# Factors of a tile copied across partition blocks by ScalarE, in place of a TensorE product with a mask

## The chip, the cores and the metric

The kernel runs on one core of one Trainium2 chip. The metric is the device time of one execution in microseconds (us). A core has five engines that work side by side, each through its own list of instructions in order: TensorE (PE; its weight loads are listed as PEld), VectorE (DVE), ScalarE (ACT), GpSimd (POOL) and SyncE (SP, which here only issues transfers). An instruction that needs another engine's result waits for it, and everything behind it on the same engine waits too. SBUF and PSUM are the on-chip memories, both with 128 partitions; matmuls write into PSUM.

## The reference, cut to what matters

The input `x` is 384 x 384 x 128 in float32. Two layers follow each other. The first is a triangle product with gates:

```python
z_n = _layernorm(z, norm_g, norm_b)              # over the 128 channels of each (row, column)
a = _linear(z_n, Wa, ba) * sigmoid(_linear(z_n, Wga, bga))
b = _linear(z_n, Wb, bb) * sigmoid(_linear(z_n, Wgb, bgb))
x = einsum('bijd,bjkd->bikd', a, b)              # per channel d a 384x384x384 product
x = _layernorm(x, normo_g, normo_b)
return z + _linear(x, Wo, bo) * sigmoid(_linear(z_n, Wgo, bgo))
```

The second layer computes gated projections of each row of that result, a sum over the row, an output projection, a residual and a layer norm. The change lies in the first layer norm, so only the first lines bear on it: every (row, column) needs a factor 1/sqrt(variance + eps), which multiplies its 128 channels before five projections.

## The kernel before, in words

The kernel has three stages. The first (to about 1280 us of the span) normalises `x`, projects it five times, and writes A and B (the factors of the triangle product), G (the output gate) and Z (the residual) to memory. The second multiplies A and B channel by channel. The third applies everything else, row by row. The change touches the first stage alone.

**Tiles and steps.** The first stage walks through 72 tiles (`NT`). A tile is 128 rows (on the partitions) by 16 columns (`CX`) by 128 channels. Each tile is worked through in four steps (`TS = 4`) of four columns (`CT = 4`); a step is called `s`, its tile `n`, its place in the tile `t` (0 to 3). The function `step(s)` writes the instructions out in this order, and no scheduler changes it: four projections `pga`, `pa`, `pgb`, `pb` of 128 x 512 on TensorE (L314), a sigmoid of `pga` and one of `pgb` on ScalarE (L322, `sga` and `sgb`), the gate of the step before on ScalarE (L264, `gt`), the two products `at` (L335) and `bt` (L351) on VectorE, the fifth projection `pgo` in four matmuls (L277), and its bias on VectorE (L279, `gs`). At the end of the step VectorE and GpSimd normalise the data of the step after next (`normalise_turned(s + 2)`, L219 and L223).

**Two ways to normalise.** The first three tiles (`OLD = 3`) are normalised with rows on the partitions and then turned by TensorE (`turn`, L249) and copied out by ScalarE (`turned_out`, L257). From tile 3 on, the kernel loads `x` a second time already turned, so that channels lie on the partitions and rows along the free axis. The mean is folded into the weights. The factor of a row must then multiply a column of the turned data, and must stand on all 128 partitions.

**How the factor gets there.** VectorE takes statistics (L160). At `t == 0` of tile `n`, GpSimd works out the factors of tile `n + 1` (`turned_factors`, L181 to L187; the last of them is a power, L187), one column of 16 factors for each row, on the partition of the row: the tile `rstd`, 128 x 16. What the later transposes need is `again`, 128 x 64: in each of the four blocks of 32 partitions, the factors of all four blocks of 32 rows. Then the 32 x 32 block transposes of VectorE (L219) yield rows along the free axis on every partition. To make `again`, GpSimd multiplies `rstd` by a mask `of_block` into `apart` (L190; each row's factor stands only in the column of its own block). In `repeat` at `t == 2`, TensorE multiplies `apart` by a constant matrix `alike` (L200; it adds up partitions that are equal modulo 32, so that every block gets all four), and ScalarE copies the 128 x 64 result from PSUM to `again` (L203). The PSUM tile is one of the two of the pool `p1t`, which the transposes `pevery` use too.

**What sets the order around it.** On ScalarE a step has `sga`, `gt`, `sgb` in this order, and at `t == 2` L203 between `gt` and `sgb`. On GpSimd a tile has, in order: the L223 product of step 0, the factors, L190, the store of G (issued at `gt`), the products of the next steps, `residual` (L242, one instruction of 4.5 us, at `t == 1`) with its store of Z, and the store of A at `t == 3`. The projections use six PSUM buffers (`p1p`) and a step uses five, so TensorE can run about one step ahead of the engines that empty them. In step 9, the first that repeats anything in the changed kernel, the turning of the old tiles still goes on: ScalarE's L257 copy of step 10's data stands at the end of step 9.

Of the kernel before, what the change touches and what calls it, by code (L numbers as in the profile page):

```python
# [9 lines left out]
FP = mybir.dt.float32  # L10
AF = mybir.ActivationFunctionType
ALU = mybir.AluOpType
# [8 lines left out]
def kernel(ctx: ExitStack, tc: tile.TileContext, ins, out: bass.AP):  # L21
# [17 lines left out]
    P = 128  # L39
# [71 lines left out]
    with tc.tile_pool(name="wprep", bufs=6) as wp, tc.tile_pool(name="p1s", bufs=3) as ps, tc.tile_pool(  # L111
# [4 lines left out]
        name="p1p", bufs=6, space=PSUM  # L116
    ) as ppp:
        tiles, turned, bts, gated, b_out_of = {}, {}, {}, {}, []
        alike = wp.tile([P, P], FP, tag="alike", name="alike", bufs=1)
        of_block = wp.tile([P, P // SQ], FP, tag="of_block", name="of_block", bufs=1)  # L120

        def place(n):
            rb, c = divmod(n, N // CX)
# [6 lines left out]
        def fetch_parts(n, parts):  # L130
            if n >= NT:
                return
            r0, c0 = place(n)
            xt = px.tile([P, CX, C], FP, tag="xt", name=f"xt_{n}")
            tiles[n] = {
                "x": xt,
                "st": ps.tile([P, CX, 6], FP, tag="st", name=f"st_{n}"),
                "rstd": ps.tile([P, CX], FP, tag="rstd", name=f"rstd_{n}"),
                "off": ps.tile([P, CX], FP, tag="off", name=f"off_{n}"),
            }  # L140
            if n < OLD:
                tiles[n]["mv"] = ps.tile([P, CX, 2], FP, tag="mv", name=f"mv_{n}")
            else:
                tiles[n]["apart"] = ps.tile([P, CX, P // SQ], FP, tag="apart", name=f"apart_{n}", bufs=1)
                tiles[n]["again"] = ps.tile([P, CX, P // SQ], FP, tag="again", name=f"again_{n}", bufs=2)
            for k in range(0, CX, CX // parts):
                nc.sync.dma_start(
                    out=xt[:, k : k + CX // parts, :], in_=x[r0 : r0 + P, c0 + k : c0 + k + CX // parts, :]
                )
                yield  # L150
# [26 lines left out]
        def turned_factors(n, c0, c1):  # L177

            st, v, d = (tiles[n][k][:, c0:c1] for k in ("st", "rstd", "off"))
            g = nc.gpsimd  # L180
            g.tensor_tensor(d, st[:, :, 1], st[:, :, 4], ALU.subtract)  # L181
            g.tensor_tensor(v, st[:, :, 2], st[:, :, 5], ALU.add)
            g.tensor_tensor(d, d, d, ALU.mult)
            g.tensor_scalar(d, d, C / 4.0, None, ALU.mult)
            g.tensor_tensor(v, v, d, ALU.add)
            g.tensor_scalar(v, v, 1.0 / C, EPS, ALU.mult, ALU.add)
            g.tensor_tensor(v, v, mhalf[:, 0 : c1 - c0], ALU.pow)  # L187
            if c1 == CX:
                v = tiles[n]["rstd"]
                g.tensor_tensor(  # L190
                    tiles[n]["apart"], v[:, :, None].to_broadcast([P, CX, P // SQ]),
                    of_block[:, None, :].to_broadcast([P, CX, P // SQ]), ALU.mult,
                )

        def repeat(n):

            if n >= NT:
                return
            again = ppt.tile([P, CT, P], FP, tag="ptr", name=f"pagain_{n}")[:, 0, 0 : CX * P // SQ]
            nc.tensor.matmul(  # L200
                again, lhsT=alike, rhs=tiles[n]["apart"].rearrange("p c b -> p (c b)"), start=True, stop=True
            )
            nc.scalar.copy(tiles[n]["again"].rearrange("p c b -> p (c b)"), again)  # L203

        def normalise_turned(s):
            n, t = divmod(s, TS)
# [86 lines left out]
        def step(s):  # L293
            n, t = divmod(s, TS)
            r0, c0 = place(n)
            if t == 0:
                if n >= OLD:
                    fetch(n + 3)
                fetch_turned(n + 2)
                if s >= CATCH_UP:  # L300
                    norm_factors(n + 1)
                tiles[n]["at"] = pa_.tile([P, CX, P], FP, tag="at", name=f"at_{n}")
                if c0 % CG == 0:
                    bts[n // TG] = (pb_ if (NT - 1 - n) // TG % 2 else pb_held).tile(
                        [P, P, CG], FP, tag="bt", name=f"bt_{n}"
                    )
            at, bt = tiles[n]["at"], bts[n // TG]
            k0 = c0 % CG + t * CT
            zT = turned[s]
            ahead = (n + 1, t - 1) if t else (n, TS - 1)  # L310

            def proj(k):
                pk = ppp.tile([P, CT, P], FP, tag="pk", name=f"p{k}_{s}")
                nc.tensor.matmul(pk, lhsT=wT[k], rhs=zT, start=True, stop=True)  # L314
                return pk

            def by_rows(p):
                return p.rearrange("d c r -> d r c")

            def sigmoid(k, pg, by_row=False):  # L320
                sg = ps.tile([P, P, CT] if by_row else [P, CT, P], FP, tag="sg", name=f"sg{k}_{s}")
                nc.scalar.activation(sg, by_rows(pg) if by_row else pg, AF.Sigmoid, bias=bcol["g" + k])  # L322
                return sg

            statistics(columns_ahead(s), columns_ahead(s + 1))
            for factors in FIRST_FACTORS.get(s, ()):
                norm_factors(*factors)
            pga, pa = proj("ga"), proj("a")
            if s == 0:
                nc.tensor.matmul(biases[:, 1, :], lhsT=nb_w, rhs=raw["go"], start=True, stop=True)  # L330
                nc.vector.tensor_tensor(gate_bias, biases[:, 1, :], gate_bias, ALU.add)
            sga = sigmoid("a", pga)
            if 0 < s <= S2:
                gate(s - 1)
            nc.vector.scalar_tensor_tensor(  # L335
                at[:, t * CT : (t + 1) * CT, :], pa, bcol["a"], sga, ALU.add, ALU.mult
            )
            if t == TS - 1:
                nc.gpsimd.dma_start(out=A[:, c0 : c0 + CX, r0 : r0 + P], in_=at)
            if t == 2 and n + 1 >= OLD:  # L340
                repeat(n + 1)
            pgb = proj("gb")
            sgb = sigmoid("b", pgb, by_row=True)
            if s + 1 < OLD * TS:
                turn(s + 1)
                turned_out(s + 1)
            if s == 0:
                normalise(0, 2)
            normalise(*ahead)
            pb = proj("b")  # L350
            nc.vector.scalar_tensor_tensor(  # L351
                bt[:, :, k0 : k0 + CT], by_rows(pb), bcol["b"], sgb, ALU.add, ALU.mult
            )
            if s < S2:
                gate_project(s)
            if s + 2 >= OLD * TS:
                normalise_turned(s + 2)
            if s < CATCH_UP:
                if s in FIRST_RESIDUALS:
                    residual(FIRST_RESIDUALS[s])  # L360
                if s in FIRST_FETCHES:
                    fetch(FIRST_FETCHES[s])
            elif t == 1:
                residual(n + 1)
            if k0 + CT == CG and n < NT - 1:
                b_out_of.extend((bt, r0, c0 + CX - CG, k) for k in range(0, P, BR))
            if t == TS - 1 and b_out_of:
                bt, r0, k0, r = b_out_of.pop(0)
                nc.sync.dma_start(out=B[:, k0 // CG, r0 + r : r0 + r + BR, :], in_=bt[:, r : r + BR, :])
# [10 lines left out]
        def of_the_turned():  # L380

            nc.vector.tensor_scalar(center, ident, -1.0 / C, None, ALU.add)
            yield
            for some in (("ga", "a"), ("gb", "b", "go")):
                centred = ppp.tile([P, CT, P], FP, tag="pk", name="centred_" + some[0])
                for n, k in enumerate(some):
                    nc.tensor.matmul(centred[:, n, :], lhsT=center, rhs=wT[k], start=True, stop=True)
                for n, k in enumerate(some):
                    nc.scalar.copy(wT[k], centred[:, n, :])
                yield  # L390
            nc.gpsimd.memset(of_block, 0.0)
            for k in range(P // SQ):
                nc.gpsimd.memset(of_block[k * SQ : (k + 1) * SQ, k : k + 1], 1.0)
            few = wp.tile([P, SQ], FP, tag="few", name="few", bufs=1)
            nc.vector.tensor_tensor(few, ident[:, 0:SQ], ident[:, SQ : 2 * SQ], ALU.add)
            for k in (2, 3):
                nc.vector.tensor_tensor(few, few, ident[:, k * SQ : (k + 1) * SQ], ALU.add)
            nc.vector.tensor_copy(
                alike.rearrange("p (b r) -> p b r", r=SQ), few[:, None, :].to_broadcast([P, P // SQ, SQ])
            )  # L400
            yield

        def last_weights():

# [661 lines left out]
```

## Time and profile before

| what | us |
|---|---|
| median of 3 runs (3215.39 to 3218.23) | 3218.12 |
| the profiled execution, its own time | 3217.2 |
| its span, first to last instruction | 3215.4 |
| TensorE busy in the span | 3184.3 |
| VectorE, GpSimd, ScalarE busy | 2714.7, 2436.2, 1793.2 |
| in the 1000 us from 300 to 1300: TensorE, VectorE, GpSimd, ScalarE busy | 994.57, 892.14, 799.21, 434.30 |
| share of the transfer engines' time in that window, GB/s | 0.92, 353 |
| granted TensorE clock | 0.998 |

How to read it: a line of a timeline gives the start in us from the start of the span, the time from the first start to the last end of what the line merges, the engine, the line of the code, the operation, output<-inputs, the shapes and the count; a bracket at the end says how long the engine had been idle just before, and what ended that. In a group of instructions, the two numbers after the count are the busy time in all and the mean duration in ns, and then the idle time before it. Durations of instructions that follow each other on one engine can overlap[...]. So the time that an engine is held by an instruction is the distance between two starts, and not the duration.

### The profile page before, as it was taken

To read this page: it belongs to the slowest core of one execution; us is meant where nothing else is said; L and a number is where in the kernel's file an instruction comes from. 1 tells how busy PE (TensorE), PEld (TensorE's weight loads), DVE (VectorE), ACT (ScalarE), POOL (GpSimd) and SP (SyncE) were. 2 spreads that over 40 slices of the span, in tenths; PEclk is the share of its full clock that TensorE was granted. 3 is DMA by queue.
4 is the path that set the end of the run, shared out by engine and by line. 5 is a ranking of instruction groups with operands and counts; after the bars stand their busy time and mean duration, and the time that the engine had idled before them with its cause. 6 is when DMAs were issued, how large, how long until landed. Compare 5 with 4: busy or idle time off the path is not lost.

```text
span 3215.4 us, 50848 instructions
## 1 busy us (share of the span) xinstructions
PE 3184.3 (99%) x14681; PEld 2103.1 (65%) x14681; DVE 2714.7 (84%) x8317; ACT 1793.2 (56%) x4190; POOL 2436.2 (76%) x2187
## 2 busy tenths in 40 slices
PE   9999999999999999999999999999999999999998
PEld 5555555555555554655555555788888888888886
DVE  7899999999999997455555555999999999999999
ACT  6444444444444444222222222588888888888888
POOL 7788888888888887455555555499999998888888
PEclk9999999999999999999999999999999999999999
DMA  6989999999999998999999999777777777777774
GB/s 236 353 342 361 366 362 365 355 360 345 368 359 363 366 355 287 368 319 313 312 311 308 311 311 303 253 254 261 272 258 261 269 261 258 270 260 259 268 264 160
DMA packets 419189, 982.72 MB, mean 306 GB/s; under 512 B 30288, under 2 KB 326352, under 8 KB 373728
## 3 DMA queue, kind: packets, MB, share of 16 engines
q1 hardware_dynamic: 377984, 752.64, 67.4%
q0 software_dynamic: 40352, 226.57, 17.8%
q8 instruction: 119, 1.95, 0.2%
q14 instruction: 158, 1.29, 0.1%
q10 hardware_dynamic: 576, 0.26, 0.0%
HBM read 526.39 MB, written 452.98 MB: 305 GB/s over the span
## 4 chain that ended last, share of the span: by engine, by line
PE 96%; POOL 1%; ACT 1%; DVE 1%; DMA 1%; issue 0%; SPq 0%; POOLq 0%; ACTq 0%; DVEq 0%
PE pm L699 23%; PE py L539 8%; PE pf L809 8%; PE pleft L835 8%; PE pg L837 8%; PE pga L314 7%; PE pgb L314 7%; PE pgo L277 7%; PE pa L314 7%; PE pb L314 7%; PE ptr L562 4%; POOL rstd L187 0%; PE pagain L200 0%; PE pg L848 0%; POOL acc L242 0%
## 5 line engine op out<-in xcount | busy, mean ns | idle before, releaser
L699 PE MATMUL pm<-ab 128*128 128x384 f32 x2304 | 745.8, 487 | 2.1 <-DVE gs L279 2.1
L719 POOL TENSOR_TENSOR acc<-acc,xd 128x384 f32<-128x384 f32 x381 | 380.8, 1000 | 362.6 <-DVE xd L712 362.4
L699 PEld LDWEIGHTS pm<-ab 128*128 128x128 f32 x2304 | 438.1, 190 | 307.3 <-DVE gs L279 2.7
L322 ACT ACTIVATE sga<-pga,c_L_conv_bga 128x512 f32<-128x512 f32 x288 | 198.0, 688 | 550.1 <-PE pga L314 550.0
L712 DVE TENSOR_TENSOR xd<-pm,acc 128x384 f32<-128x384 f32 x381 | 212.2, 557 | 344.2 <-POOL acc L719 320.1
L717 ACT ACTIVATE sq<-xd 128x384 f32<-128x384 f32 x381 | 188.5, 495 | 541.2 <-DVE xd L712 541.1
L827 ACT ACTIVATE res<-res,off,rs 128x128 f32<-128x128 f32 x1134 | 474.8, 485 | 1.4
L545 DVE SCALAR_TENSOR_TENSOR py<-py,acc,gr 128x128 f32<-128x128 f32 x1152 | 416.7, 362 | 0.9
L277 PEld LDWEIGHTS pgo<-wT_go,xT 128*128 128x128 f32 x2208 | 287.5, 192 | 124.8 <-issue 78.9
L550 DVE BATCH_NORM_STATS2 st<-res 128x6 f32<-128x128 f32 x1128 | 338.8, 300 | 0.0
L860 POOL TENSOR_TENSOR res<-res,r_L_conv_ln_bias 128x1536 f32<-128x1536 f32 (+1 forms) x96 | 326.7, 3403 | 7.5
L859 POOL TENSOR_TENSOR res<-res,r_L_conv_ln_scale 128x1536 f32<-128x1536 f32 (+1 forms) x96 | 326.9, 3406 | 0.7 <-ACT res L827 0.5
L242 POOL TENSOR_TENSOR acc<-xt,r_L_conv_b_out 128x2048 f32<-128x2048 f32 x72 | 326.5, 4535 | 0.0
L223 POOL TENSOR_TENSOR xT<-every,xT 128x256 f32<-128x256 f32 x276 | 202.6, 734 | 155.3 <-DVE every L219 152.1
L539 PE MATMUL py<-w_o,xr 128*128 128x128 f32 x2304 | 320.0, 275 | 0.0
L809 PE MATMUL pf<-w_o,h 128*128 128x128 f32 x2280 | 316.7, 275 | 0.0
L835 PE MATMUL pleft<-pairT,m_L_conv_W_left 128*128 128x384 f32 x768 | 311.5, 487 | 0.4 <-ACT pairT L563 0.4
L837 PE MATMUL pg<-pairT,m_L_conv_W_gate 128*128 128x384 f32 x768 | 310.6, 486 | 0.0
L842 ACT ACTIVATE sg<-pg,c_L_conv_b_gate 128x384 f32<-128x384 f32 x384 | 223.2, 581 | 150.4 <-PE pg L837 101.5
L351 DVE SCALAR_TENSOR_TENSOR bt<-pb,c_L_conv_bb,sgb 128x512 f32<-128x512 f32 x288 | 216.2, 751 | 97.3 <-PE pb L314 93.2
L314 PE MATMUL pga<-xT,wT_ga 128*128 128x512 f32 x552 | 284.0, 596 | 7.6 <-POOL xT L223 7.5
L539 PEld LDWEIGHTS py<-w_o,xr 128*128 128x128 f32 x2304 | 288.4, 192 | 0.8
(195 smaller groups left out, 6537.7 us busy)
## 6 DMA issues: line engine op xcount, KB each, us to landing
Z<-acc POOLq DMA_DIRECT2D x72, 1024.0 KB, 10.4
A<-at POOLq DMA_DIRECT2D x72, 1024.0 KB, 14.1
G<-gt POOLq DMA_DIRECT2D x72, 1024.0 KB, 10.2
gr<-G SPq DMA_DIRECT2D x96, 768.0 KB, 5.8
zr<-Z SPq DMA_DIRECT2D x96, 768.0 KB, 7.3
xr<-X SPq DMA_DIRECT2D x96, 768.0 KB, 8.2
X<-xd SPq DMA_DIRECT2D x381, 192.0 KB, 5.7
xt<-in_x_dram SPq DMA_DIRECT2D x71, 1024.0 KB, 7.5
```

Of the source, the lines that this page charges most:

```text
L277: nc.tensor.matmul(pgo[:, c, :], lhsT=zT[:, c, :], rhs=wT["go"], start=True, stop=True)
L314: nc.tensor.matmul(pk, lhsT=wT[k], rhs=zT, start=True, stop=True)
L539: nc.tensor.matmul(py[:, q, :], lhsT=g["x"][:, i, q * P : (q + 1) * P], rhs=w_o0, start=True, stop=True)
L545: nc.vector.scalar_tensor_tensor(py[:, q, :], py[:, q, :], rs0[:, q, u : u + 1], g["g"][:, i, q, :], ALU.mult, ALU.mult)
L550: nc.vector.bn_stats(b["st"][:, k, q, :], b["res"][:, k, q, :])
L699: nc.tensor.matmul(products[d, ib].rearrange("p (s c) -> p s c", c=CG), lhsT=ab[:, 0, q, ib * P : (ib + 1) * P], rhs=b_of(d)[:, :, q, :], ...
L719: nc.gpsimd.tensor_tensor(s1[:, ib, :], s1[:, ib, :], xd, ALU.add)
L809: nc.tensor.matmul(pf[:, q, :], lhsT=h[:, q * P : (q + 1) * P], rhs=w_o, start=True, stop=True)
L827: nc.scalar.activation(g["res"][:, i, q, :], g["res"][:, i, q, :], AF.Identity, bias=g["off"][:, i, q : q + 1], scale=g["rs"][:, i, q : q ...
L835: nc.tensor.matmul(pleft, lhsT=w_left, rhs=pairT, start=True, stop=True)
L837: nc.tensor.matmul(pg[:, 0:N], lhsT=w_gate, rhs=pairT, start=True, stop=True)
L859: nc.gpsimd.tensor_tensor(flat, flat, over(ln_s, n * NB), ALU.mult)
```

## The change

`apart`, `of_block` and `alike` go, with the instructions that make them. `repeat` copies on ScalarE instead: for each of the four blocks of 32 rows and each of the four blocks of 32 partitions, one copy of 32 partitions x 16 elements from `rstd` to a strided place in `again`, sixteen in a tile. It moves from `t == 2`, ahead of the third projection, to `t == 1`, behind the sigmoid `sgb`. In program order it then stands ahead of `turn(s + 1)` and `turned_out(s + 1)` where a step still has them. Only the first of the sixteen copies waits (for GpSimd's `rstd`); the other fifteen wait for nothing.

```diff
@@ norm_factors / turned_factors
             g.tensor_tensor(v, v, mhalf[:, 0 : c1 - c0], ALU.pow)
-            if c1 == CX:
-                v = tiles[n]["rstd"]
-                g.tensor_tensor(
-                    tiles[n]["apart"], v[:, :, None].to_broadcast([P, CX, P // SQ]),
-                    of_block[:, None, :].to_broadcast([P, CX, P // SQ]), ALU.mult,
-                )
 
         def repeat(n):
 
             if n >= NT:
                 return
-            again = ppt.tile([P, CT, P], FP, tag="ptr", name=f"pagain_{n}")[:, 0, 0 : CX * P // SQ]
-            nc.tensor.matmul(
-                again, lhsT=alike, rhs=tiles[n]["apart"].rearrange("p c b -> p (c b)"), start=True, stop=True
-            )
-            nc.scalar.copy(tiles[n]["again"].rearrange("p c b -> p (c b)"), again)
+            for b in range(P // SQ):
+                for to in range(P // SQ):
+                    nc.scalar.copy(
+                        tiles[n]["again"][to * SQ : (to + 1) * SQ, :, b], tiles[n]["rstd"][b * SQ : (b + 1) * SQ, :]
+                    )
@@ step
-            if t == 2 and n + 1 >= OLD:
-                repeat(n + 1)
             pgb = proj("gb")
             sgb = sigmoid("b", pgb, by_row=True)
+            if t == 1 and n + 1 >= OLD:
+                repeat(n + 1)
             if s + 1 < OLD * TS:
                 turn(s + 1)
                 turned_out(s + 1)
@@ of_the_turned
                 for n, k in enumerate(some):
                     nc.scalar.copy(wT[k], centred[:, n, :])
                 yield
-            nc.gpsimd.memset(of_block, 0.0)
-            for k in range(P // SQ):
-                nc.gpsimd.memset(of_block[k * SQ : (k + 1) * SQ, k : k + 1], 1.0)
-            few = wp.tile([P, SQ], FP, tag="few", name="few", bufs=1)
-            nc.vector.tensor_tensor(few, ident[:, 0:SQ], ident[:, SQ : 2 * SQ], ALU.add)
-            for k in (2, 3):
-                nc.vector.tensor_tensor(few, few, ident[:, k * SQ : (k + 1) * SQ], ALU.add)
-            nc.vector.tensor_copy(
-                alike.rearrange("p (b r) -> p b r", r=SQ), few[:, None, :].to_broadcast([P, P // SQ, SQ])
-            )
-            yield
```

More of the change, by code (lines that the diff above doesn't have):

```diff
@@ L118 @@
         tiles, turned, bts, gated, b_out_of = {}, {}, {}, {}, []
-        alike = wp.tile([P, P], FP, tag="alike", name="alike", bufs=1)
-        of_block = wp.tile([P, P // SQ], FP, tag="of_block", name="of_block", bufs=1)
         def place(n):
@@ L143, in fetch_parts @@
             else:
-                tiles[n]["apart"] = ps.tile([P, CX, P // SQ], FP, tag="apart", name=f"apart_{n}", bufs=1)
                 tiles[n]["again"] = ps.tile([P, CX, P // SQ], FP, tag="again", name=f"again_{n}", bufs=2)
```

## The prediction, made before the changed kernel ran

> **What bounds the kernel now.** I read the page first (who is busy in the stage that the change touches), then the chain that ended last, then one tile of the first stage engine by engine.
>
> ```profile
> PE 96%; POOL 1%; ACT 1%; DVE 1%; DMA 1%; issue 0%; SPq 0%; POOLq 0%; ACTq 0%; DVEq 0%
> ```
>
> TensorE holds the end of the program: whatever makes its list shorter in the first stage shows in full, unless a wait takes its place. Now one tile of the first stage, TensorE's timeline:
>
> ```profile
> 608.58 1.02 PE L314 MATMUL pga<-xT,wT_ga 128*128 128x512 f32 x2
> ...
> 612.91 1.02 PE L314 MATMUL pga<-xT,wT_ga 128*128 128x512 f32 x2
> 613.77 1.02 PE L314 MATMUL pa<-xT,wT_a 128*128 128x512 f32 x2
> 614.62 0.33 PE L200 MATMUL pagain<-apart,alike 128*128 128x64 f32 x2
> 614.79 1.08 PE L314 MATMUL pgb<-xT,wT_gb 128*128 128x512 f32 x2
> ...
> 617.46 1.02 PE L314 MATMUL pga<-xT,wT_ga 128*128 128x512 f32 x2
> ```
>
> A plain step lasts 612.91 - 608.58 = 4.33 us, with no gap. The step with L200 lasts 617.46 - 612.91 = 4.55 us. So L200 costs TensorE 0.22 us in each tile, on the path. ScalarE in the same steps:
>
> ```profile
> 611.36 0.69 ACT L322 ACTIVATE sgb<-pgb,c_L_conv_bgb 128x512 f32<-128x512 f32 x1 [0.45 <-PE pgb L314]
> 614.03 0.69 ACT L322 ACTIVATE sga<-pga,c_L_conv_bga 128x512 f32<-128x512 f32 x1 [1.98 <-PE pga L314]
> 614.61 0.62 ACT L264 ACTIVATE gt<-gs 128x512 f32<-128x512 f32 x1
> 615.13 0.20 ACT L203 COPY again<-pagain 128x64 f32<-128x64 f32 x1
> 615.91 0.69 ACT L322 ACTIVATE sgb<-pgb,c_L_conv_bgb 128x512 f32<-128x512 f32 x1 [0.57 <-PE pgb L314]
> ```
>
> The new copies follow the `sgb` at 611.36 (`t == 1`). ScalarE is idle 1.98 us there, then waits for TensorE again: it has 2.4 us of spare time in a step. GpSimd:
>
> ```profile
> 607.90 2.94 POOL L187 TENSOR_TENSOR rstd<-rstd,mhalf 128x16 f32<-128x16 f32 x1
> 610.91 0.29 POOL L190 TENSOR_TENSOR apart<-rstd,of_block 128x64 f32<-128x64 f32 x1
> 611.15 0.64 POOL L267 DMA_DIRECT2D G<-gt  x1
> 611.81 0.74 POOL L223 TENSOR_TENSOR xT<-every,xT 128x256 f32<-128x256 f32 x1
> 614.23 0.73 POOL L223 TENSOR_TENSOR xT<-every,xT 128x256 f32<-128x256 f32 x1 [1.67 <-DVE every L219]
> ```
>
> The product at 611.81 ends at 612.55, and TensorE needs it at 612.91: GpSimd is only 0.36 us ahead at `t == 2`. That is the tightest place beside TensorE's own.
>
> **The change part by part.**
>
> *L200 goes.* 0.22 us in each of the 66 tiles in which TensorE sets the pace: -14.5 us. In the last three tiles (no fifth projection there, it comes later) TensorE waits for GpSimd's L223, so there only GpSimd's gain counts.
>
> *L190 goes.* It holds GpSimd some 0.27 us (it lasts 0.29, and the next starts 0.24 after it). In most tiles that is cover: the 0.36 us become 0.6. On the path it counts where TensorE waits for the L223 behind it: two early tiles (waits of 1.88 us at 82.13 and 1.64 us at 156.56) and the last three (1.04 and 0.94 us in two of them). 5 x 0.27 = -1.3 us.
>
> *The setup goes* (five memsets and four VectorE instructions, 1.4 us in all, near 53 us). VectorE's next product there starts without a wait, TensorE's step 7 is not held by it: 0. *L203 and the PSUM buffer go*: ScalarE had time, and `pevery` loses a neighbour: 0.
>
> *Sixteen copies come, per tile.* The trace has no ScalarE instruction on 32 partitions, so I bound one. Nearest in shape is a 128x16 activation, SBUF to SBUF:
>
> ```profile
> 3197.02 0.22 ACT L995 ACTIVATE root<-ident 128x16 f32<-128x16 f32 x1
> 3197.14 1.25 ACT L827 ACTIVATE res<-res,off,rs 128x128 f32<-128x128 f32 x3
> ```
>
> The next starts 0.12 us after it, though it lasts 0.217 us: lower end 16 x 0.122 = 1.95 us. The Trainium skill has a rule against it: "VectorE: DVE Perf Modes", section "Two Vector instructions with no wait between them", says that a VectorE instruction whose output starts in another block of 32 partitions than the last one's starts only when all earlier ones are finished. The copies change that block every time. The rule is for VectorE; no run here shows whether ScalarE does it. If so, nothing overlaps: 16 x 0.217 = 3.5 us, and with the lost overlap of 0.095 us as a new start cost besides, 16 x 0.31 = 5.0 us, an estimate. So 1.95 to 5.0. I take 1.95, the row, since the rule names another engine.
>
> *What 1.95 or 3.5 us do.* The copies start when `sgb` lets go, 611.36 + 0.58 (the distance from `sga` to `gt`) = 611.94. GpSimd's power has ended at 610.84, so the first copy doesn't wait; in nearly all tiles the power is 1.2 us ahead. They end at 613.9 or 615.4; `sga`, next in the queue, was due at 614.03. At 3.5 it is 1.4 us late. VectorE's `at` waits for it, but stands at 615.64 anyway, and `sga` ends by 616.1: 0.5 us late. TensorE needs `at` only when its buffer comes round, at `pgb` of the next step, 2.5 us after `at` normally ends. `again` is needed first by L219 at 618.0. So both are hidden.
>
> *Where it stops being hidden.* Let the copies take C. Then `sgb` of `t == 2` ends at 613.7 + C, and behind it on VectorE stand `bt`, `gs`, three instructions of L219/L223, the statistics, `at` and so on with hardly a gap: by start distances the L219 for the product that GpSimd does ahead of the factors ends at about 619.4 + C. From there GpSimd needs 0.7 (product), 1.6 (six small ones), 2.9 (power), 0.7 (store of G) and 0.8 (product) = 6.8 us, to 626.2 + C. TensorE wants that product at 612.91 + 4 x 4.33 = 630.2. So up to C = 4.0 us (0.25 us a copy) TensorE sees nothing; each us beyond can cost up to a us a tile.
>
> *The one place without cover: step 9.* The first copies (tile 3) stand ahead of ScalarE's copy of step 10's data:
>
> ```profile
> 59.42 1.67 POOL L187 TENSOR_TENSOR rstd<-rstd,mhalf 128x8 f32<-128x8 f32 x1
> 59.89 0.58 ACT L257 COPY zn<-ptr 128x512 f32<-128x512 f32 x1
> ...
> 61.23 1.02 PE L314 MATMUL pga<-zn,wT_ga 128*128 128x512 f32 x2
> ```
>
> L257 ran at 59.89. Now ScalarE waits for the power's end at 61.09, copies for 1.95, and only then does L257 (0.58): TensorE's `pga` starts at 61.15 + 1.95 + 0.58 + 0.08 = 63.76 in place of 61.23, +2.5 us (+4.1 at 3.5). GpSimd's chain behind waits for VectorE's L219 of step 10, which follows TensorE, so nothing gives this back.
>
> *Sum:* -14.5 - 1.3 + 2.5 = -13.3 us against the profiled execution's 3217.2 (its span is 3215.4, the rest lies around it unchanged): 3203.9. The median lies 0.9 above: 3204.8. With C = 3.5 it would be 3206.4. Prediction: 3205.
>
> **The rivals.**
>
> *The copies cost 0.3 us each (slower).* ScalarE restarts from nothing at each block change, so C = 4.8, and the wait moves through VectorE to GpSimd's factors and TensorE's `pga` at `t == 2`. 0.8 us beyond the 4.0; since a stalled TensorE also moves the next tile's deadline back, I count half: 66 x 0.4 = +26, step 9 adds 5.4 in all: 3218 - 14.5 - 1.3 + 5.4 + 26 = 3234. For it: the rule above; ScalarE's copies here write three other blocks and come back, sixteen times. Against: 0.31 needs both the full 0.217 and a start cost. It decides from 0.28 us a copy on.
>
> *Another engine sets the pace (no change).* The transfer engines are busy for 0.92 of the window at 353 GB/s; a tile moves six times 1 MB in 17.53 us. If that rate is a ceiling, tiles stay at 17.53 us, and only the start's +2.5 and the last tiles' gain remain: 3219. Against it: slices of the same window move up to 412 GB/s, and TensorE's chain has no wait for a transfer. Copies at 0.27 to 0.29 us land here too.
>
> *GpSimd is late with the factors*, and ScalarE waits at the first copy with `sga` and `gt` behind it. Four of 69 tiles have the power after `sgb`, by up to 1.1 us, and in these TensorE was stalled by GpSimd already: at most +3 us, 3208, inside the forecast.
>
> **How the numbers follow.** A measurement of this kernel tells about 0.2%, 6.4 us, from no change: faster is under 3211.7, slower over 3224.6. Copies under 0.26 us with the pace still TensorE's: 66%, 3202 to 3211. No change (ceiling, or copies near 0.28): 12%. Slower (copies of 0.29 and over): 22%, of which about half lies under 3235. The range reaches from a start that is given back (3202 less 1) into that case: 3201 to 3234; the likeliest case alone has 3202 to 3209.
>
> **What would show it.** Right: plain steps of 4.33 us at every `t`, tiles of 17.32; copies starting 0.12 us apart; `sga` after them at once or up to 1.5 us late; `pga` of step 10 some 2.5 us later; L223 ahead of `pga` at `t == 2` with 0.6 us to spare. Wrong: copies starting 0.25 us or more apart, VectorE waiting for `sgb` at `t == 2`, TensorE waiting for GpSimd's L223 in the middle tiles, or tiles that stay at 17.5 us with nothing but transfers behind.

## The result, and the profile after

| | median us | ratio to before, 95% interval |
|---|---|---|
| before | 3218.18 (6 runs, 3215.39 to 3219.32) | |
| changed | 3206.01 (6 runs, 3205.59 to 3206.82) | 0.9964 [0.9953, 0.9974] |

The changed kernel is faster by 12.2 us; the forecast was 3205. The profiled execution took 3205.72 us, with a span of 3203.9 against 3215.4. The total fits. The terms fit less well, as the traces show.

TensorE in the middle of the first stage of the changed kernel (its timeline; the places of the code have moved: L305 is the projections, L268 the fifth one, L313 the sigmoids, L192 the copies, L210 and L214 the transposes and products that normalise, L326 `at`):

```profile
607.15 1.02 PE L305 MATMUL pga<-xT,wT_ga 128*128 128x512 f32 x2
...
611.48 1.02 PE L305 MATMUL pga<-xT,wT_ga 128*128 128x512 f32 x2
...
615.80 1.02 PE L305 MATMUL pga<-xT,wT_ga 128*128 128x512 f32 x2
```

Both steps last 4.33 us; the 0.22 us of the removed product are gone, with no gap in their place. ScalarE in the same steps (`t == 1`, then `t == 2`):

```profile
609.93 0.69 ACT L313 ACTIVATE sgb<-pgb,c_L_conv_bgb 128x512 f32<-128x512 f32 x1 [0.45 <-PE pgb L305]
610.51 3.62 ACT L192 COPY again<-rstd 32x16 f32<-32x16 f32 x16
614.16 0.69 ACT L313 ACTIVATE sga<-pga,c_L_conv_bga 128x512 f32<-128x512 f32 x1
614.74 0.62 ACT L255 ACTIVATE gt<-gs 128x512 f32<-128x512 f32 x1
615.26 0.68 ACT L313 ACTIVATE sgb<-pgb,c_L_conv_bgb 128x512 f32<-128x512 f32 x1
616.92 0.69 ACT L313 ACTIVATE sga<-pga,c_L_conv_bga 128x512 f32<-128x512 f32 x1 [0.98 <-PE pga L305]
```

The sixteen copies take 3.62 us, not the 1.95 I chose. The starts in the trace lie 0.228 us apart, and one lasts 0.217: each waits for the one before. `sga` follows at once at 614.16, 1.56 us late: in a step in which ScalarE waits it starts 1.12 us after `pga`, here at 612.60. One step later ScalarE waits for TensorE again. VectorE waits for it at `at`:

```profile
614.88 0.75 DVE L326 SCALAR_TENSOR_TENSOR at<-pa,c_L_conv_ba,sga 128x512 f32<-128x512 f32 x1 [0.58 <-ACT sga L313]
```

GpSimd, in the stretch that the prediction called the tightest:

```profile
606.88 2.93 POOL L184 TENSOR_TENSOR rstd<-rstd,mhalf 128x16 f32<-128x16 f32 x1
609.78 0.64 POOL L258 DMA_DIRECT2D G<-gt  x1
610.45 0.74 POOL L214 TENSOR_TENSOR xT<-every,xT 128x256 f32<-128x256 f32 x1
612.80 0.72 POOL L214 TENSOR_TENSOR xT<-every,xT 128x256 f32<-128x256 f32 x1 [1.61 <-DVE every L210]
```

The product ends at 611.19 and TensorE starts at 611.48: 0.29 us to spare. But this tile is one of the tightest. The next one is the common case:

```profile
627.49 0.74 POOL L214 TENSOR_TENSOR xT<-every,xT 128x256 f32<-128x256 f32 x1
628.78 1.02 PE L305 MATMUL pga<-xT,wT_ga 128*128 128x512 f32 x2
```

Here the product ends at 628.23, 0.55 us ahead. Of the 61 tiles from step 32 to step 276, 56 have 0.53 to 0.70 us to spare, four have 0.28 or 0.29, and the last waits. In the kernel before, the middle value was 0.34. So the margin has grown, almost to the 0.6 us forecast.

And the start. TensorE's timeline of the changed kernel around step 10, and its waits in the first 300 us (us in all, times, longest):

```profile
60.92 1.05 PE L268 MATMUL pgo<-wT_go,zn 128*128 128x128 f32 x8
65.94 1.27 PE L305 MATMUL pga<-zn,wT_ga 128*128 128x512 f32 x2 [3.96 <-ACT zn L248]
67.00 1.91 PE L305 MATMUL pa<-zn,wT_a 128*128 128x512 f32 x2
68.71 1.77 PE L305 MATMUL pgb<-zn,wT_gb 128*128 128x512 f32 x2
70.31 0.60 PE L240 MATMUL ptr<-ident,zn 128*128 128x128 f32 x4
70.75 1.02 PE L305 MATMUL pb<-zn,wT_b 128*128 128x512 f32 x2
```

```profile
PE pga L305 <- ACT zn L248: 4.0, 1, 4.0
PE pga L305 <- POOL xT L214: 3.2, 3, 1.3
```

TensorE waits 3.96 us for the copy of the turned data, as the prediction said of this place. But then the projections start 1.06 to 1.71 us apart and not 0.86: the granted clock is 0.50 from 67 to 70 us, as the table by stretches of the changed kernel shows (columns: length of the stretch, TensorE busy, its weight loads, VectorE, ScalarE, GpSimd, granted clock, share of the transfer engines, GB/s):

```profile
64.00:67.00 3.00, 1.06 (x2) 0.49 (x3) 0.00 (x0) 1.80 (x7) 2.70 (x2) 0.96 0.00 0
67.00:70.00 3.00, 3.00 (x5) 1.23 (x4) 0.75 (x1) 1.21 (x2) 0.02 (x1) 0.50 0.94 235
70.00:74.00 4.00, 4.00 (x19) 2.47 (x18) 2.05 (x4) 1.60 (x3) 0.17 (x1) 0.98 0.95 338
```

Where the 11.5 us of the span went, from the starts of `pga` (and of the second stage's `pm`) in the two traces:

| stretch | before | changed | difference |
|---|---|---|---|
| steps 0 to 8 | 41.49 | 42.12 | +0.6 |
| steps 8 to 12 (the first copies) | 18.85 | 24.55 | +5.7 |
| steps 12 to 32 | 94.99 | 93.11 | -1.9 |
| steps 32 to 276 (61 tiles) | 1068.45 | 1054.19 | -14.3 |
| steps 276 to 287 (the last tiles) | 41.10 | 41.20 | +0.1 |
| second stage, first to last `pm` | 748.79 | 747.05 | -1.7 |
| from there to the end | 1173.82 | 1173.84 | 0.0 |

The 1.7 us of the second stage are the clock too, this time in the kernel before:

```profile
1297.00:1300.40 3.40, 3.40 (x7) 1.72 (x6) 0.00 (x0) 0.16 (x1) 2.53 (x3) 0.51 0.93 340
```

That is the kernel before, after a wait of 2.11 us at 1296.38. The changed kernel waits 1.98 us at the same place and keeps its full clock:

```profile
1287.00:1290.40 3.40, 3.40 (x12) 2.01 (x11) 0.00 (x0) 0.27 (x1) 2.42 (x3) 1.00 0.94 354
```

Seven matmuls in 3.4 us in one, twelve in the other.

### The profile page after: what moved, and what is told of

Read it like the earlier page. It is cut to its first block, busy times and chain, and to the rows that moved or that the text cites. A ratio compares the mean times of both kernels' runs of the same rounds, so it can differ in the third digit from the quotient of the medians.

```text
span 3203.9 us, 51462 instructions
## 1 busy us (share of the span) xinstructions
PE 3168.4 (99%) x14543; PEld 2086.5 (65%) x14543; DVE 2703.2 (84%) x8313; ACT 2009.0 (63%) x5225; POOL 2414.4 (75%) x2113
## 4 chain that ended last, share of the span: by engine, by line
PE 95%; DMA 2%; POOL 1%; ACT 1%; issue 1%; DVE 1%; SPq 0%; ACTq 0%; POOLq 0%; DVEq 0%
PE pm L679 23%; PE py L519 8%; PE pf L789 8%; PE pleft L815 8%; PE pg L817 8%; PE pgo L268 7%; PE pga L305 7%; PE pa L305 7%; PE pgb L305 7%; PE pb L305 7%; PE ptr L542 4%; DMA B<-bt 1%; PE pg L828 0%; POOL acc L233 0%; DMA xt<-in_x_dram 0%
## 5 line engine op out<-in xcount | busy, mean ns | idle before, releaser
L525 DVE SCALAR_TENSOR_TENSOR py<-py,acc,gr 128x128 f32<-128x128 f32 x1152 | 452.9, 393 | 0.9 <-PE py L519 0.2
L313 ACT ACTIVATE sga<-pga,c_L_conv_bga 128x512 f32<-128x512 f32 x288 | 197.9, 687 | 347.3 <-PE pga L305 345.6
L530 DVE BATCH_NORM_STATS2 st<-res 128x6 f32<-128x128 f32 x1128 | 375.3, 333 | 0.0
L268 PEld LDWEIGHTS pgo<-wT_go,xT 128*128 128x128 f32 x2208 | 287.5, 192 | 124.8 <-issue 78.4
L214 POOL TENSOR_TENSOR xT<-every,xT 128x256 f32<-128x256 f32 x276 | 202.0, 732 | 150.1 <-DVE every L210 144.4
L305 PE MATMUL pga<-xT,wT_ga 128*128 128x512 f32 x552 | 284.1, 596 | 6.7 <-POOL xT L214 6.5
L268 PE MATMUL pgo<-wT_go,xT 128*128 128x128 f32 x2208 | 288.5, 275 | 0.0
## 6 DMA issues: line engine op xcount, KB each, us to landing
A<-at POOLq DMA_DIRECT2D x72, 1024.0 KB, 13.4
```

Of the source, the lines that this page charges most:

```text
L268: nc.tensor.matmul(pgo[:, c, :], lhsT=zT[:, c, :], rhs=wT["go"], start=True, stop=True)
L525: nc.vector.scalar_tensor_tensor(py[:, q, :], py[:, q, :], rs0[:, q, u : u + 1], g["g"][:, i, q, :], ALU.mult, ALU.mult)
L530: nc.vector.bn_stats(b["st"][:, k, q, :], b["res"][:, k, q, :])
```

## The experiments

**Why a copy costs 0.23 us.** Two kernels tell. In the first, each copy stays in its own block of partitions, so that three of four columns of `again` hold wrong factors. Only the loops and the input differ:

```diff
-            for b in range(P // SQ):
-                for to in range(P // SQ):
+            for to in range(P // SQ):
+                for b in range(P // SQ):
                     nc.scalar.copy(
-                        tiles[n]["again"][to * SQ : (to + 1) * SQ, :, b], tiles[n]["rstd"][b * SQ : (b + 1) * SQ, :]
+                        tiles[n]["again"][to * SQ : (to + 1) * SQ, :, b], tiles[n]["rstd"][to * SQ : (to + 1) * SQ, :]
                     )
```

> Sixteen copies of 32x16 as before, but each from a block of 32 partitions to the same block, four in a row (the wrong factors stand in three of four columns). Theory (a copy that starts in another block than the one before it waits until that one is finished): 12 of 15 distances fall to 0.12 us, 3 stay at 0.23, so the sixteen take 12 x 0.12 + 3 x 0.23 + 0.22 = 2.4 us in place of 3.6. Rival (a copy of 32 partitions with a strided output takes 0.23 us wherever it starts): 3.6 us, as in the changed kernel.

Measured: 3203.78 us in one run.

```profile
608.57 2.14 ACT L192 COPY again<-rstd 32x16 f32<-32x16 f32 x16
```

In the trace the starts lie 0.105 us apart inside a block (0.12 was expected) and 0.22 to 0.23 us apart at the three changes of block. The size, the number of partitions and the stride of the output are the same as in the changed kernel, so they are not what costs. Nor is it that a copy crosses from one block to another: none of the copies here does, and the three changes of block still cost 0.22 to 0.23 us. Semaphores do not explain the distances either: of the fifteen copies behind the first, the trace of the changed kernel names one for a single copy at most, and that copy is no later than the others (0.227 us).

The second keeps the right factors and swaps the two loops alone:

```diff
-            for b in range(P // SQ):
-                for to in range(P // SQ):
+            for to in range(P // SQ):
+                for b in range(P // SQ):
```

> The same sixteen copies in another order: the output's block stays for four copies, the input's changes with each. Theory (a change of either block makes the copy wait): 3.6 us for the sixteen, as before. Rival (only the output's block counts): 2.4 us.

Measured: 3205.51 us in one run, and

```profile
610.40 3.63 ACT L192 COPY again<-rstd 32x16 f32<-32x16 f32 x16
```

Here the output stays in a block for four copies and only the input moves: still 3.63 us. In the changed kernel only the output moves, except every fourth time. So a change on either side is enough.

**The start.** The copies stand behind the copy of the turned data, which matters in step 9 alone:

```diff
-            if t == 1 and n + 1 >= OLD:
-                repeat(n + 1)
             if s + 1 < OLD * TS:
                 turn(s + 1)
                 turned_out(s + 1)
+            if t == 1 and n + 1 >= OLD:
+                repeat(n + 1)
```

> The copies stand behind the copy of the turned data in step 9 (the one step where both are there); all other steps are unchanged. Theory (the start's loss is real and nothing gives it back): the stall of 4.0 us ahead of step 10 goes, and with it the slower TensorE clock of step 10 (1.8 us); the next copy of turned data, at the end of step 10, comes about 1 us late instead. 3206.0 - 5.9 + 1 = 3201. Rival (GpSimd sets the pace of steps 10 to 15 anyway and gives the stall back): 3206.

Measured: 3201.16 us (3200.11 to 3202.97), ratio 0.9949 [0.9935, 0.9962]. Steps 8 to 12 take 19.76 us in place of 24.55, and steps 12 to 32 are the same within 0.15 us. Its timeline:

```profile
65.41 1.05 PE L268 MATMUL pgo<-wT_go,zn 128*128 128x128 f32 x8
67.34 1.13 PE L305 MATMUL pga<-zn,wT_ga 128*128 128x512 f32 x2 [0.87 <-ACT zn L248]
68.30 1.02 PE L305 MATMUL pa<-zn,wT_a 128*128 128x512 f32 x2
```

The long stall and the half clock are gone (from 5 to 3186 us of this trace it is never below 1.00), a wait of 0.87 us one step later has come. Nothing later gives the loss back, which was the rival.

**TensorE's 0.22 us alone.** A product of the removed one's size returns to its old place, with nothing that reads it:

```diff
+            if t == 2 and OLD <= n + 1 < NT:
+                dead = ppt.tile([P, CT, P], FP, tag="ptr", name=f"dead_{n}")[:, 0, 0 : CX * P // SQ]
+                nc.tensor.matmul(dead, lhsT=ident, rhs=ident[:, 0 : CX * P // SQ], start=True, stop=True)
             pgb = proj("gb")
```

> The changed kernel with a TensorE product of the size of the one removed (128x64, weights of 128x128, into the same PSUM pool) at its old place at t == 2; nothing reads it. Theory (the gain is TensorE's 0.22 us a tile): +14.5 us, 3220. Rival (TensorE has slack beside late VectorE and GpSimd in the changed kernel): 3206.

Measured: 3220.5 us (3218.85 to 3223.14), ratio to before 1.0009 [1.0000, 1.0017]. The 61 middle tiles take 1067.03 us, 12.8 more than in the changed kernel: 0.21 us a tile. (The two profiled executions are 13.4 us apart, the medians 14.5.) So without this saving the change would not gain at all.

**GpSimd's product alone.** It returns to its place behind the power, again unread (a tile for it is added too):

```diff
             g.tensor_tensor(v, v, mhalf[:, 0 : c1 - c0], ALU.pow)
+            if c1 == CX:
+                v = tiles[n]["rstd"]
+                g.tensor_tensor(
+                    tiles[n]["apart"], v[:, :, None].to_broadcast([P, CX, P // SQ]),
+                    mhalf[:, None, 0 : P // SQ].to_broadcast([P, CX, P // SQ]), ALU.mult,
+                )
```

> The changed kernel with GpSimd's product of 128x64 put back into its place behind the power, with nothing that reads it. Theory (the gain is TensorE's 0.22 us a tile; GpSimd's 0.29 us count only in the tiles where TensorE waits for GpSimd): 1 to 2 us slower than the changed kernel, 3207.5. Rival (GpSimd's 20 us are the gain): 3218. Between them, if the late VectorE has used up GpSimd's spare time: each tile loses up to 0.2 us, 3220.

Measured: 3210.6 us (3209.14 to 3211.48), ratio 0.9976 [0.9966, 0.9986], 4.6 us over the changed kernel. That lies between the first value and the third. In the traces, 2.7 us of it are in the middle tiles and 1.0 in steps 12 to 32. Another 0.9 us lie in step 10, where the clock stays at 0.50 for 6.8 us in this trace and for 3.4 in that of the changed kernel; those are not GpSimd's time. In most middle tiles some 0.2 us are left to spare, in ten of the 61 nothing. In one of these the product ends at 614.56 (613.82 + 0.74) and TensorE, due at 614.50, starts at 614.61:

```profile
612.91 0.29 POOL L188 TENSOR_TENSOR apart<-rstd,mhalf 128x64 f32<-128x64 f32 x1
613.15 0.64 POOL L265 DMA_DIRECT2D G<-gt  x1
613.82 0.74 POOL L221 TENSOR_TENSOR xT<-every,xT 128x256 f32<-128x256 f32 x1
```

So beside late copies, GpSimd's 0.27 us are no longer all cover: they are paid for in the tightest tiles.

**Where the copies stop being hidden.** Four, then eight copies more behind the sixteen (the same with `range(8)`):

```diff
+            for k in range(4):
+                to = k % (P // SQ)
+                nc.scalar.copy(
+                    tiles[n]["again"][to * SQ : (to + 1) * SQ, :, 3], tiles[n]["rstd"][3 * SQ : 4 * SQ, :]
+                )
```

> Four copies more in each tile behind the sixteen (they write one column again): 20 x 0.228 = 4.55 us. Theory (the delay is hidden until GpSimd's product at t == 2 is late; the changed kernel has 0.29 us to spare there with 3.64 us of copies, so the limit is at 3.93): 0.62 us beyond it in each tile, counted between a half and the whole, 66 x 0.31 to 0.62 = 20 to 41, and 0.9 at step 9: 3227 to 3248. Rival (copies cost nothing as long as ScalarE's spare time of a tile, some 9 us, is not used up): 3207.

> Eight copies more in each tile: 24 x 0.228 = 5.46 us. Theory: 1.53 us beyond the limit of 3.93, a half to the whole in each of 66 tiles, 50 to 101, and 1.8 at step 9: 3258 to 3309. Rival (ScalarE's spare time of a tile counts): 3208.

Measured: 3228.64 us (3227.82 to 3231.28), ratio 1.0037 [1.0022, 1.0051], and 3280.75 us (3280.7 to 3281.2), ratio 1.0197 [1.0182, 1.0213]. The copies take 4.63 and 5.61 us, a little more than expected: each of the added ones waits for a semaphore and starts 0.24 us behind the one before. The middle tiles lose (1072.89 - 1054.19) / 61 = 0.31 us each with 20 copies and (1120.45 - 1054.19) / 61 = 1.09 us with 24. So the last 0.98 us of copies cost 0.78 us a tile. The waits between 300 and 1220 us of the kernel with 24 copies show the chain:

```profile
DVE at L331 <- ACT sga L318: 126.8, 51, 2.7
```

```profile
POOL A L335 <- DVE at L331: 76.2, 46, 1.7
```

```profile
PE pga L310 <- POOL xT L219: 33.2, 50, 0.9
```

ScalarE is late with `sga`, VectorE with `at`, GpSimd with what follows, and at last TensorE waits for GpSimd's product, once a tile. GpSimd waits for `at` at its store of A; but what ends last ahead of its factors is VectorE's transpose, as the prediction had it:

```profile
620.20 0.72 POOL L219 TENSOR_TENSOR xT<-every,xT 128x256 f32<-128x256 f32 x1 [0.18 <-DVE every L215]
```

ScalarE still waits for TensorE at other steps of the same tile, so its spare time is there and does not help:

```profile
ACT sga L318 <- PE pga L310: 161.8, 100, 2.0
```

**The place.** The same copies one step later:

```diff
-            if t == 1 and n + 1 >= OLD:
+            if t == 2 and n + 1 >= OLD:
                 repeat(n + 1)
```

> The sixteen copies one step later, behind the sigmoid of t == 2. Theory: they end 1.9 us after VectorE wants them, VectorE is 1.4 us late at the product ahead of GpSimd's factors and TensorE waits up to 0.8 us a tile at the next t == 2, half of it counted: +26 (up to +53); the stall at step 9 (5.9 with the slower clock) turns into one of some 3.5 at step 10: 3230, between 3215 and 3257. Rival (VectorE's spare time of 1.9 us a tile hides it): 3203.

Measured: 3270.37 us (3267.29 to 3273.15), ratio 1.0165 [1.0150, 1.0180], outside what was expected, on the dear side. The waits in the same stretch:

```profile
DVE every L210 <- ACT again L192: 94.2, 50, 2.2
```

```profile
PE pga L305 <- POOL xT L214: 34.1, 51, 0.9
```

VectorE waits 1.88 us a tile (1.9 was expected), and TensorE waits for GpSimd's product as described. The size was wrong: a middle tile loses (1115.78 - 1054.19) / 61 = 1.0 us, where I had counted half of 0.8. The halving is no rule.

**Fewer copies.** The last run joins the better start with six copies: four into the first block of partitions, then blocks to blocks (the added lines; the loops of the sixteen go):

```diff
+            again = tiles[n]["again"]
+            for b in range(P // SQ):
+                nc.scalar.copy(again[0:SQ, :, b], tiles[n]["rstd"][b * SQ : (b + 1) * SQ, :])
+            for to in (SQ, 2 * SQ):
+                nc.scalar.copy(again[to : 2 * to], again[0:to])
```

> The version with the copies behind the turned data (3201.2), and six copies in place of sixteen: four of 32x16 into the first block, then the first block to the second (32x64) and the first two to the last two (64x64). They should take 4 x 0.23 and twice about 0.3 with the wait for the copy before: 1.5 us in place of 3.6. Theory (from 4 us down the copies cost nothing in the middle tiles; what is left of them is the 0.9 us ahead of step 11 and some tenths in the last tiles): 3200. Rival (VectorE's lateness still costs in the middle tiles): 3195 or less.

Measured: 3200.2 us (3199.84 to 3201.53), ratio 0.9948 [0.9935, 0.9962].

```profile
604.55 0.89 ACT L192 COPY again<-rstd 32x16 f32<-32x16 f32 x4
605.47 0.52 ACT L194 COPY again<-again 32x64 f32<-32x64 f32 x2
```

They take 1.44 us. The middle tiles take 1054.20 us, as with sixteen copies: the rival is out. GpSimd's product is now 0.70 us ahead in most of them, so the late copies cost 0.15 us of margin and no time. The wait ahead of step 11 is gone (steps 8 to 12: 18.62 us), but in this trace steps 0 to 8 and the second stage give some tenths back, and the medians, 1 us apart with ranges that overlap, don't tell this version from the one with sixteen. Both beat the two kernels of this case.

## Why the prediction was right, point by point

*L200 goes, -14.5.* Right, and shown alone: putting an equal product back costs 14.5 us (3220.5 against 3206.0).

*L190 goes, -1.3, elsewhere it widens GpSimd's cover to 0.6 us.* The cover is 0.55 us in most middle tiles and 0.29 in the tightest ones. With the product put back the kernel is 4.6 us slower, of which some 3.7 are GpSimd's: its 0.27 us were needed in ten of the middle tiles and in two early ones (0.6 and 0.4 us less in these). In the last tiles the gain did not come at all (-0.8 foreseen, +0.1 measured): TensorE waits less at `t == 2` and more at the next `t == 0`. That VectorE's lateness moves the wait there is my reading; no run took it apart.

*The setup goes, 0.* Right. Steps 0 to 8 are 0.6 us longer in the changed trace, between 0.2 and 0.9 in those of the other runs, but all of it lies in step 0, where TensorE waits 1.71 us for VectorE's tile `r_L_conv_bgo` and waited 1.08 before. Steps 1 to 8 take 35.18 us in both traces. What makes that wait vary was not tried.

*Sixteen copies, 1.95 us.* This choice was wrong. The measured 3.62 us is the value of the rule that I weighed and set aside (3.5): "VectorE: DVE Perf Modes", section "Two Vector instructions with no wait between them" of the Trainium skill. It is written for VectorE. The two kernels of the first experiment show ScalarE doing the same, for input and output: 0.228 us against 0.105. The nearest row (0.122) was near in size and far in the one property that decided. The upper end, a start cost on top of the full duration, did not occur: 0.228 is 0.217 and 0.01.

*Hidden in the middle tiles.* Right at both values, as the text said, and this is why the wrong choice cost little.

*The limit at C = 4.0 us.* Right in place, and near in size: at 3.63 us no tile loses, at 4.63 each loses 0.31. Where TensorE waits for the product it starts 0.05 us behind it, so some 0.50 of the 0.55 us are free in most tiles and 0.24 in the tightest. If each further us of copies takes a us of margin, the limit is 4.1 us, and 3.9 in those four tiles: an estimate, no run stands between. The 0.29 us from which the expectation for 20 copies started was the tightest tiles' margin.

*Step 9, +2.5, or +4.1 at 3.5.* Step 9 is 4.1 us longer (the wait is 3.96) where I took 2.5, from the mis-sized C. Behind it lies a term that I didn't have: the clock halves for 3.4 us, and step 10 takes 6.56 us where 4.77 were due without the product, +1.8. Together 5.9, and the version with the other order gets 4.9 of it back, having a wait of its own.

*The sum.* The start came out 3.4 us dearer than forecast (5.9 against 2.5), the last tiles 0.9 and the first step 0.6. Against that, the middle gave 0.8 us more than its 61 x 0.22, and the second stage 1.7 us, by a clock that happened to stay up. So the 3205 owes its fit to errors that cancel. The sign, and some 10 us of the size, rest on the 0.22 us a tile.

## What to carry to other kernels

Copies that hop between blocks of partitions are serial on ScalarE (0.228 us each here, against 0.105 inside a block): count their full duration, or write to one block and double from there. A delay on an engine with time to spare is to be followed through the lists of the others to the first deadline; that deadline, and not the spare time, is the limit, and here it stood about half a us away. And look at the first place where a moved instruction stands ahead of something that the bounding engine needs at once: one such step cost a third of what the change saved.

## What the runs showed that I had not expected

TensorE's clock falls to 0.50 after a wait: for 3.4 us behind the 3.96 us of the changed kernel (1.8 us lost), and behind only 2.11 us in the kernel before at the entry to the second stage (1.7 us lost), while 1.98 us at the same place left it at 1.00. With 20 or 24 copies, and with GpSimd's product put back, the slow stretch at the start lasted 6.8 us.

The traces of this case show what decides. In all eleven, each stretch between two changes of the clock is a whole multiple of 3.413 us: in the changed kernel 61.44 us (18 of them) at full clock, then one at half. Laid along this grid, the two waits look different. First the kernel before, then the changed one (columns as above):

```profile
1293.67:1297.09 3.42, 1.31 (x4) 0.49 (x3) 1.61 (x3) 2.12 (x4) 0.53 (x1) 1.00 1.09 256
```

```profile
1281.93:1285.34 3.41, 2.58 (x16) 1.70 (x14) 2.48 (x4) 1.85 (x5) 0.53 (x1) 1.00 1.10 312
1285.34:1288.75 3.41, 2.26 (x7) 1.44 (x8) 0.69 (x1) 1.93 (x4) 0.77 (x2) 1.00 0.87 301
```

The wait of 2.11 us lies inside one window of 3.41 us. The wait of 1.98 us is split by a boundary into 0.83 and 1.15 us. In the eleven traces every full-clock window with 2.11 us or more of idle TensorE (22, half of them at the end of the program) is followed by half clock, and none with 1.84 us or less is. A slow window with 0.95 to 1.91 us idle is followed by another slow one; behind one without idle time the clock is back. So what counts is the idle time within a window, and where the boundaries fall decides what a wait of some 2 us costs. Where the limit lies between 1.84 and 2.11 us stays open, and the idle times rest on the profile's modelled ends of the matmuls.

The Trainium skill ("TensorE: Matmul & The Clock Gate", section "Part 1: The HAM clock gate") ties the halving to an idle window of about 3.4 us, and says that the windows run freely. The length of the slow stretch and the grid agree; but a window that was idle for 2.11 of its 3.41 us was enough.
